# One branch, joined act-table loads and a shorter clear in a convolution, attention and recurrence kernel

## The chip, the cores and the metric

The kernel runs on one core of a Trainium2 chip. The core has five engines with a queue of instructions each: TensorE (PE, matrix products; PEld is its weight load), VectorE (DVE), ScalarE (ACT), GpSimd (POOL) and SyncE (SP, which here issues most DMA transfers). The metric is the device time of one execution in microseconds (us), lower is better. Times of before and after are medians over timed runs; profiles are of one execution each.

## The reference

Input x has 32 images of 128 channels and 64 by 64 positions. Two layers follow each other.

```
# layer 0
x = x + conv3x3(groupnorm(x), kernel mixed per image from 4 kernels)
# layer 1, t = tokens of x, 4096 per image, 128 features
t = t + attn(ln(t))          # 128 -> 16 features, windows of 144 with stride 72, 4 heads,
                             # back to 128, gated, then a layer norm
t = t + ffn(ln(t))

def ffn(x):                  # batch norm over all images, then a recurrence over the tokens
    Wx = x @ W.T
    Wx = (Wx - mean(Wx)) * rsqrt(var(Wx) + 1e-5) * gamma + beta
    y_t = sigmoid(Wx_t + y_(t-1) @ V.T)
```

The mean and variance of the batch norm run over all 32 images, so the recurrence can start only when the last image's `Wx` has its statistics.

## The kernel before

**Start.** Constants are built, image 0 is loaded, and bounds on the inputs are checked on the chip: `okf` says that the attention scores are small enough for an exponential without a maximum, `vm` that the matrix V is contracting enough for the recurrence to be cut into independent runs. Both become integers (`oki` at line 389, `okv` at line 398) and are loaded into registers (lines 426 and 429). The four convolution kernels are loaded into the tiles `k0` by SP at line 318, ahead of the branch; `k0` lives in a pool `first` of its own.

**First branch (line 1984).** If the scores are small, `images` runs, otherwise `images_by_shift`, a slower path that these inputs don't take. `images` works through the 32 images with jobs per image: load (statistics, the mixed kernel `h`), waves (nine buffers `u` of row differences for a fast convolution, on POOL and DVE), taps (transformed kernels `w`), conv (PE products of `w` and `u`), drain, project, feed, values, attend (scores `sc`, exponentials `ex`, weighted values `av`), divide, tail (layer norm and the first result) and last (second layer norm, product with `fWc`, statistics `bnmv`, and the store of the result to `z_d`). Each job is a generator that yields the engine and the tiles that its next step needs. A planner in the kernel keeps a clock of its own (class `Clock`) for each engine; it takes the step that can begin first, and among equals the one with the earliest due time, which the table `DUE` gives per job as (start, length, number of steps) in units of an image. Where the planner expects PE to wait for long, it puts in filler products of `fWc` with itself. So the order of the instructions on all engines follows from the planner's clock and `DUE`. All of these instructions are recorded at line 243.

The tiles `place` (five of 4.6 KB per partition, four of them `k0`) receive kernels, broadcast rows of statistics and squares in turn. In the last image's `last` job the variances are turned into reciprocal deviations on ACT (Ln, Exp), eight products with `fWc` are copied out by ACT (`zt<-nm`), and then PE broadcasts the deviations (`sc<-place,once`) for DVE, which scales and takes the statistics.

**Join, scale, second branch.** Behind the join the batch norm's scale `scl` and shift `shf` are worked out in small steps (lines 1999 to 2011): DVE gathers means and variances, ACT takes the square root, DVE finishes. A second branch (line 2214) takes `by_runs` if V is contracting, otherwise `by_steps`.

**`by_runs`.** Each image's 4096 steps are cut into 128 runs of 32 steps, each warmed up over 16 steps of the run before. Two images form a group, four groups are under way at a time as streams. SP loads the groups' `zr` tiles from `z_d` (line 2033; group 0 lies in `frames` already), DVE builds `dg`, the diagonal of `scl` (line 2041), and clears the state tiles `yw`, two per stream (line 2060). Then each step is a product with V (line 2102), an addition of the input by PE (line 2090) or DVE (line 2108), and a sigmoid (line 2113; the first step of a stream is line 2115). In the warm-up steps only columns 1 to 127 of `yw` are written and read, column 0 stays as cleared. POOL puts the states into `zr`, which is added to the output by DMA.

Of the kernel before, what the change touches and what calls it, by code (L numbers as in the profile page):

```python
# [8 lines left out]
F32 = mybir.dt.float32  # L9
AF = mybir.ActivationFunctionType  # L10
ALU = mybir.AluOpType
AX = mybir.AxisListType

P = 128
# [5 lines left out]
NK = 4  # L20
# [6 lines left out]
GT = NWG * WIN  # L27
# [9 lines left out]
NI = 2  # L37
# [2 lines left out]

SPARE = 0.3, 0.6, 0.6
DUE = {
    "setup": (0.32, 0.08, 8),
    "load": (-0.91, 0.63, 29),
    "taps": (0.02, 0.22, 6),
    "waves": (-0.25, 0.4, 26),
    "conv": (-0.45, 1.09, 36),
    "drain": (-9.0, 0.0, 14),
    "project": (0.75, 0.37, 33),
    "feed": (1.72, 0.61, 27),  # L50
    "values": (1.43, 1.03, 28),
    "attend": (1.15, 1.27, 71),
    "divide0": (1.92, 0.02, 15),
    "divide1": (2.34, 0.02, 11),
# [204 lines left out]
def hybrid_kernel(  # L259
# [24 lines left out]
    nc = tc.nc  # L284
# [17 lines left out]
        return t  # L302


    early = ExitStack()
    first = early.enter_context(tc.tile_pool(name="first", bufs=1))
    inorder = ExitStack()
    inorder.enter_context(tc.manual_schedule())
    tmp = inorder.enter_context(tc.tile_pool(name="tmp", bufs=1))
# [1 line left out]
    frames = const.tile([P, NI, (H + 2) * (W + 2)], F32, name="frames")  # L311
    framed = frames[:, :, 0:T]
    x0 = frames[:, 0].rearrange("p (h w) -> p h w", w=W + 2)[:, 1 : H + 1, 1 : W + 1]
    k0 = [first.tile([P, 9 * P], F32, name=f"place{k}") for k in range(NK)]
    for i in range(2):
        nc.sync.dma_start(x0[:, 32 * i : 32 * i + 32], x[0, :, 32 * i : 32 * i + 32, :])
    for k in range(NK):
        nc.sync.dma_start(k0[k], conv_k[:, k].rearrange("m i j l -> m (i j l)"))

    bdr = tmp.tile([P, DK], F32, name="bdr")  # L320
    ipr = tmp.tile([P, 3 * DK], F32, name="ipr")
# [24 lines left out]

    okf = const.tile([P, 1], F32, name="okf")
    oki = const.tile([P, 1], mybir.dt.int32, name="oki")
    okv = const.tile([P, 1], mybir.dt.int32, name="okv")
    st0 = tmp.tile([P, NBLK, 6], F32, name="st0")  # L350
    mv0 = first.tile([P, 2], F32, name="mv0")
    ps1 = inorder.enter_context(tc.tile_pool(name="ps1", bufs=1, space=bass.MemoryType.PSUM))

    def stats0(i0, i1):
# [31 lines left out]
    smx = tmp.tile([P, 1], F32, name="smx")  # L386
    nc.vector.tensor_reduce(smx, sm, axis=AX.X, op=ALU.max)
    nc.vector.tensor_scalar(okf, smx, 60.0 / HD**-0.5, None, ALU.is_le)
    nc.vector.tensor_copy(oki, okf)
    vr = tmp.tile([P, 1], F32, name="vr")  # L390
    nc.vector.tensor_reduce(vr, va_, axis=AX.X, op=ALU.add)
    vt_ = ps1.tile([P, P], F32, name="vt_")
# [2 lines left out]
    vm = tmp.tile([P, 1], F32, name="vm")  # L395
    nc.vector.tensor_reduce(vm, vt_, axis=AX.X, op=ALU.max)
    nc.vector.tensor_scalar(vm, vm, 1.02, None, ALU.is_le)
    nc.vector.tensor_copy(okv, vm)
    stats0(4, NBLK)
    nc.vector.bn_aggr(mv0, st0.rearrange("p i s -> p (i s)"))  # L400

# [21 lines left out]
    ghalf = const.tile([P, 1], F32, name="ghalf")  # L423
    nc.vector.tensor_scalar_mul(ghalf, gsig, 0.5)
    inorder.close()
    contr = nc.values_load(okv[0:1, 0:1], min_val=0, max_val=1)

    bnmv = const.tile([P, NB, 2], F32, name="bnmv")
    small = nc.values_load(oki[0:1, 0:1], min_val=0, max_val=1)


    QT, NPL, NF, NZ, NU = T // 4, 5, 2, 3, 9
# [1 line left out]
    def images(nc):  # L434
# [6 lines left out]
        with ExitStack() as pa:  # L441
# [26 lines left out]
            def kept(shape, name, fill=None):  # L468
                t = keep.tile(shape, F32, name=name)
                if fill is not None:  # L470
                    nc.gpsimd.memset(t, fill)
                return t
# [18 lines left out]
                nc.vector.tensor_mul(dst, dst, l)  # L491


            places = k0 + [kept([P, 9 * P], f"place{i}") for i in range(NK, NPL)]
            spare = list(places)

            def spread(jobs):
# [139 lines left out]
            def load(b):  # L637
# [11 lines left out]
                taps = []  # L649

                def kernel():
                    if b == 0:
                        taps.append(spare.pop(0))
                        return
                    w = yield from place("SP", ())
                    nc.sync.dma_start(w, conv_k[:, len(taps)].rearrange("m i j l -> m (i j l)"))
                    taps.append(w)
# [679 lines left out]
            def last(b):  # L1337

                while ("x2", b, 0) not in done or (b and ("tail", b - 1) not in done):
                    yield  # L1340
                zt = done["proj", b]

                def product(h):

                    for i in range(4 * h, 4 * h + 4):
                        s = slice(i * BLK, (i + 1) * BLK)
                        yield "PE", nms, (zt[:, s],), (zw[:, s],)
                        ps = clock.take("PE", nms)
                        nc.tensor.matmul(ps, fWc, zt[:, s], start=True, stop=True)
                        yield "ACT", None, (ps,), (zw[:, s],), True  # L1350
                        nc.scalar.copy(zw[:, s], ps)
                        nms.append(ps)

                def third(i):
                    z = zt[:, quarter(i)]

                    def use(w):
                        nc.vector.tensor_mul(z, z, w[:, 0:QT])
                        for j in range(2):
                            nc.vector.bn_stats(st[:, 2 * i + j, :], z[:, BLK * j : BLK * (j + 1)])  # L1360

                    return r_d[b, 2, 1, quarter(i)].partition_broadcast(P), (z,), use

                def straight(i, w):
                    z = zw[:, quarter(i)]
                    zu = z.rearrange("p (g r t) -> p r g t", r=4, t=32)
                    nc.vector.tensor_mul(zu, zu, w)
                    for j in range(2):
                        nc.vector.bn_stats(st[:, 2 * i + j, :], z[:, BLK * j : BLK * (j + 1)])

                got = yield from deviations(zt[:, 0:T], b, 2, True, lambda c: ("x2", b, c))
                st = sml.tile([P, NBLK, 6], F32, name="st3")
                zw = zt
                if b == NB - 1:
                    zw = big.tile([P, T + 8], F32, name="zt")
                    for h in range(2):
                        yield from product(h)
                    yield from beam(got, straight)
                for h in range(2):
                    if b < NB - 1:  # L1380
                        yield from product(h)
                        yield from spread(third(i) for i in (2 * h, 2 * h + 1))
                    yield "SP", None, (zw[:, part(h)],)
                    nc.sync.dma_start(z_d[b, :, part(h)], zw[:, part(h)])
                nc.vector.bn_aggr(bnmv[:, b, :], st.rearrange("p i s -> p (i s)"))
                done["tail", b] = True
# [171 lines left out]
    def images_by_shift():  # L1558

        with ExitStack() as pa:  # L1560
# [126 lines left out]
            def front(b):  # L1687
# [43 lines left out]
                nc.vector.tensor_reduce(cs, co, axis=AX.X, op=ALU.add)  # L1731
                nc.vector.reciprocal(cs, cs)
                nc.vector.tensor_scalar_mul(co, co, cs)
                wb = k0[0].rearrange("p (k m) -> p k m", k=9)
                nc.vector.tensor_scalar_mul(wb, kT[:, 0], co[:, 0:1])
                for k in range(1, NK):
                    nc.vector.scalar_tensor_tensor(
# [28 lines left out]
            def attention(zt):  # L1766
# [25 lines left out]
                for g in range(8):  # L1792
# [77 lines left out]
                        s = slice(GH * i, GH * i + n)  # L1870
                        nc.vector.tensor_add(qs[:, s], qs[:, s], ps[:, i, 0:n])

                    av = k0[2 + q % 2][:, 0:GT]
                    for m0 in range(0, nw, 3):
                        ms = range(m0, min(m0 + 3, nw))
                        ap = av_tile()
# [46 lines left out]
                    for i in range(8):  # L1923
# [2 lines left out]
                            on[:n, i].rearrange("p h f -> p (h f)"),  # L1926
                            ident[:n, :n],
                        )
                    oc = k0[1][:NG5, 0:GT]
                    nc.scalar.copy(  # L1930
                        oc[:, 0:nt].rearrange("p (a b) -> p a b", a=2), ps[:NG5, :, 0 : 4 * n]
                    )
# [48 lines left out]
                tail(b, *cur)  # L1981
                cur = nxt

    with tc.If(small > 0) as arm:
        images(nc)
    with arm.Else():
        images_by_shift()
        for i in range(NI):
            nc.sync.dma_start(framed[:, i], z_d[i])
    early.close()  # L1990


    scl = const.tile([P, 1], F32, name="scl")
    shf = const.tile([P, 1], F32, name="shf")
    bmv = const.tile([P, 2], F32, name="bmv")

    bms = const.tile([P, 6], F32, name="bms")
    bma = const.tile([P, NB], F32, name="bma")
    nc.vector.tensor_copy(bma, bnmv[:, :, 0])
    nc.vector.bn_stats(bms, bma)  # L2000
    nc.vector.bn_aggr(bmv, bms)
    bva = const.tile([P, 1], F32, name="bva")
    nc.vector.tensor_reduce(bva, bnmv[:, :, 1], axis=AX.X, op=ALU.add)
    nc.vector.scalar_tensor_tensor(
        bmv[:, 1:2], bva, 1.0 / NB, bmv[:, 1:2], ALU.mult, ALU.add
    )
    nc.scalar.activation(scl, bmv[:, 1:2], AF.Sqrt, bias=eps)
    nc.vector.reciprocal(scl, scl)
    nc.vector.tensor_mul(scl, scl, fg)
    nc.vector.tensor_mul(shf, bmv[:, 0:1], scl)  # L2010
    nc.vector.tensor_sub(shf, fb, shf)

    def by_runs():

# [2 lines left out]
        with ExitStack() as pb:  # L2017
            zp = pb.enter_context(tc.tile_pool(name="zp", bufs=NSTR + 1))
            hp = pb.enter_context(tc.tile_pool(name="hp", bufs=1))
            p_v = pb.enter_context(tc.tile_pool(name="p_v", bufs=2, space=bass.MemoryType.PSUM))  # L2020
            pb.enter_context(tc.manual_schedule())

            NG = NB // NI
            zs = {}
# [25 lines left out]
            class Stream:  # L2050

                def __init__(self, j):
                    self.j, self.g, self.k, self.phase = j, j, 0, "ACT"
                    self.at = 10.0 * j
                    self.ahead = self.ps = None
                    self.read, self.kept = [-9.0, -9.0], [-9.0, -9.0]
                    self.yw = []
                    for i in range(2):
                        self.yw.append(hp.tile([P, NI, NRUN], F32, name=f"yw{j}_{i}"))
                        nc.vector.memset(self.yw[i], 0.0)  # L2060

                def step(self, k):
                    warm = k < WARM
# [98 lines left out]
    def by_steps():  # L2162

        with ExitStack() as pb:
            fix = pb.enter_context(tc.tile_pool(name="fix", bufs=1))
            io = pb.enter_context(tc.tile_pool(name="io", bufs=2))
            p_s = pb.enter_context(tc.tile_pool(name="p_s", bufs=3, space=bass.MemoryType.PSUM))
            dg = fix.tile([P, P], F32, name="dg")
            nc.vector.tensor_scalar_mul(dg, ident, scl)
            y0 = fix.tile([P, NB], F32, name="y0")  # L2170
# [40 lines left out]
                nc.vector.tensor_add(xk, xk, yk.rearrange("p t b -> p b t"))  # L2211
                nc.sync.dma_start(of[:, :, k * CH : (k + 1) * CH], xk)

    with tc.If(contr > 0) as arm:
        by_runs()
    with arm.Else():
        by_steps()


# [52 lines left out]
```

## Time and profile before

| what | us |
|---|---|
| timed runs | 4437.79, 4440.0, 4445.95 (median 4440.0) |
| the profiled execution | 4430.95 |
| its span, first to last instruction | 4429.2 |
| PE's first convolution product | starts at 36.51 |
| the last image's statistics done | 3877.58 |
| the recurrence's first sigmoid | 3887.83 |
| last copy of POOL before the final DMA | 4399.9 |

A line of the timeline gives the start, the length, the engine, the line, the operation with its output and inputs, and in square brackets how long the engine stood idle before it and what ended that. PE's mean granted clock in this execution is 0.982 of full speed.

### The profile page before, as it was taken

The numbers are of one execution on the slowest core, as the hardware profiler recorded it, in microseconds if no ns is written. First come the engines' busy times: TensorE is split into PE (matmuls) and PEld (weight loads), VectorE is DVE, ScalarE is ACT, GpSimd is POOL, SyncE is SP. The second block draws the span as 40 slices with busy tenths as digits, with TensorE's granted clock in tenths as the row PEclk, the third lists the DMA queues.
The fourth block names the chain that finished last, engine by engine and source line by source line (L and its number), as shares of the span: only waits on it lengthen the run. The fifth ranks groups of instructions, "written<-read, shape, count | busy, mean of one in ns | idle before, by whom it ended". The sixth has DMA issues, their size and how long they took to land.

```text
span 4429.2 us, 103395 instructions
## 1 busy us (share of the span) xinstructions
PE 4151.1 (94%) x42569; PEld 2150.3 (49%) x42569; DVE 3558.9 (80%) x5378; ACT 2423.2 (55%) x3500; POOL 1675.1 (38%) x1654
## 2 busy tenths in 40 slices
PE   6999999999999999999999999999999999889986
PEld 3554544445444544444544545444444445555443
DVE  8788888888888887887887878888888866759884
ACT  1455555555555555555554555555555456467774
POOL 3343333333333333333333333333333422037665
PEclk9999999999999999999999999999999999999998
DMA  3435555545554655555554555555555534459998
GB/s 107 141 116 170 174 177 184 187 166 173 185 168 151 194 174 168 172 180 180 169 179 133 185 171 179 168 168 173 185 185 182 174 119 163 173 204 262 287 264 171
DMA packets 455885, 782.10 MB, mean 177 GB/s; under 512 B 327436, under 2 KB 337380, under 8 KB 422756
## 3 DMA queue, kind: packets, MB, share of 16 engines
q1 hardware_dynamic: 444788, 708.03, 49.0%
q0 software_dynamic: 8704, 67.11, 7.4%
q8 instruction: 339, 5.55, 0.5%
q14 instruction: 150, 1.23, 0.1%
q10 hardware_dynamic: 1904, 0.18, 0.0%
HBM read 494.22 MB, written 274.43 MB: 174 GB/s over the span
## 4 chain that ended last, share of the span: by engine, by line
PE 55%; DVE 21%; DMA 12%; issue 4%; ACT 3%; POOL 2%; SPq 2%; DVEq 0%; ACTq 0%; POOLq 0%
PE nm L243 31%; PE sc L243 12%; PE av L243 9%; DVE zt L243 6%; DVE v L2108 3%; PE v L2102 3%; DVE frames L243 2%; DMA place<-x_d 2%; ACT ex L243 2%; DMA out_dram<-zr 2%; DMA zr<-z_d 2%; DVE u L243 2%; SPq L243 2%; DMA place<-r_d 2%; DVE h L243 2%
## 5 line engine op out<-in xcount | busy, mean ns | idle before, releaser
L243 ACT ACTIVATE ex<-sc 128x1728 f32<-128x1728 f32 x672 | 1081.9, 1610 | 718.9 <-PE sc L243 712.5
L243 POOL TENSOR_TENSOR qe<-qs,mqk 128x576 f32<-128x576 f32 x448 | 615.3, 1376 | 931.4 <-PE sc L243 930.6
L243 PE MATMUL nm<-u,w 128*128 128x512 f32 x1536 | 786.0, 628 | 21.2 <-POOL w L243 18.7
L243 PE MATMUL sc<-qe,ks 32*128 32x432 f32 (+1 forms) x7168 | 667.9, 442 | 33.6 <-ACT ex L243 17.8
L243 PE MATMUL av<-ex,VE 128*32 128x144 f32 x14336 | 620.5, 291 | 21.9 <-DVE avs L243 21.4
L243 PEld LDWEIGHTS av<-ex,VE 128*32 128x32 f32 x14336 | 390.4, 109 | 332.5 <-issue 242.5
L243 PEld LDWEIGHTS sc<-qe,ks 32*128 32x128 f32 x7168 | 285.5, 184 | 414.9 <-issue 185.7
L2102 PE MATMUL v<-yw,fVT 128*128 128x254 f32 (+1 forms) x1504 | 436.3, 429 | 35.5 <-ACT yw L2115 26.1
L243 POOL TENSOR_TENSOR u<-frames 128x528 f32<-128x528 f32 x256 | 383.1, 1505 | 101.5 <-PE nm L243 98.9
L2113 ACT ACTIVATE yw<-v,shf 128x254 f32<-128x254 f32 (+1 forms) x752 | 354.0, 473 | 121.3 <-DVE v L2108 49.4
L2108 DVE SCALAR_TENSOR_TENSOR v<-zr,scl,v 128x256 f32<-128x256 f32 (+1 forms) x585 | 346.2, 659 | 91.7 <-PE v L2102 91.3
L243 PEld LDWEIGHTS nm<-u,w 128*128 128x128 f32 x1536 | 265.4, 192 | 313.5 <-issue 278.3
L243 PE MATMUL nm<-u,h 128*128 128x512 f32 x768 | 399.6, 627 | 0.8 <-DVE frames L243 0.8
L2102 PEld LDWEIGHTS v<-yw,fVT 128*128 128x128 f32 x1504 | 242.0, 194 | 243.5 <-ACT yw L2113 192.1
L243 ACT ACTIVATE place<-zt 128x1024 f32<-128x1024 f32 x256 | 266.5, 1054 | 151.6 <-DVE zt L243 136.1
L243 DVE SCALAR_TENSOR_TENSOR u<-u,u 128x528 f32<-128x528 f32 x256 | 247.9, 982 | 51.9 <-POOL u L243 50.2
L2119 POOL COPY zr<-yw 128x256 f32<-128x256 f32 x416 | 256.2, 728 | 86.8 <-ACT yw L2113 86.2
L243 PE MATMUL nm<-zt,fWc 128*128 128x512 f32 x512 | 273.7, 630 | 3.4 <-ACT zt L243 2.0
L243 PE MATMUL nm<-place,avg 128*32 128x256 f32 x3072 | 237.2, 383 | 12.9 <-ACT place L243 12.6
L243 POOL TENSOR_TENSOR kt<-ks,mqk 128x384 f32<-128x384 f32 (+1 forms) x96 | 88.0, 917 | 389.8 <-ACT ks L243 325.7
L243 ACT COPY zt<-nm 128x512 f32<-128x512 f32 x256 | 149.0, 584 | 152.5 <-PE nm L243 150.6
L243 DVE COPY avs<-av 128x288 f32<-128x288 f32 x224 | 100.8, 450 | 156.5 <-PE av L243 155.6
(226 smaller groups left out, 6417.5 us busy)
## 6 DMA issues: line engine op xcount, KB each, us to landing
place<-r_d SPq DMA_DIRECT2D x380, 512.0 KB
place<-in_conv_k_dram SPq DMA_DIRECT2D x128, 576.0 KB
out_dram<-zt SPq DMA_DIRECT2D x64, 1024.0 KB
z_d<-zt SPq DMA_DIRECT2D x64, 1024.0 KB
x_d<-frames SPq DMA_DIRECT2D x31, 2112.0 KB
place<-x_d SPq DMA_DIRECT2D x124, 528.0 KB
frames<-in_x_dram SPq DMA_DIRECT2D x124, 512.0 KB
zr<-z_d SPq DMA_DIRECT2D x26, 2048.0 KB
```

Of the source, the lines that this page charges most:

```text
L243: got = f(*args, **kw)
L2102: nc.tensor.matmul(self.ps[:, :, c], fVT, self.yw[1 - r % 2][:, :, c], start=not whole, stop=True)
L2108: nc.vector.scalar_tensor_tensor(v, z, scl, v, ALU.mult, ALU.add)
L2113: nc.scalar.activation(y[:, :, c], self.ps[:, :, c], AF.Sigmoid, bias=shf)
L2119: nc.gpsimd.tensor_copy(z, y)
```

## The change

The two flags become one: `vm` is multiplied by `okf` and only the product is turned into an integer. One branch is left, at the end. Its first arm is `images` followed by `by_runs`, its second `images_by_shift` followed by `by_steps`; the scale is worked out at the head of each recurrence in a function `scale`. The pool `first` goes: all five `place` tiles are now the images' own, so image 0's kernels are loaded inside the branch, by the `load` job. ACT's table for the square root is loaded in the last image's `last` job, behind the deviations, and the sigmoid's right behind the square root. Of each `yw` tile only column 0 is cleared. Four rows of `DUE` have other values. (The paths that these inputs don't take get tiles of their own instead of `k0`.)

```diff
 DUE = {
-    "setup": (0.32, 0.08, 8),
+    "setup": (-0.12, 0.02, 8),
-    "waves": (-0.25, 0.4, 26),
-    "conv": (-0.45, 1.09, 36),
+    "waves": (0.02, 0.09, 26),
+    "conv": (-0.35, 1.1, 36),
-    "values": (1.43, 1.03, 28),
+    "values": (1.41, 1.09, 28),
...
-    early = ExitStack()
-    first = early.enter_context(tc.tile_pool(name="first", bufs=1))
...
-    k0 = [first.tile([P, 9 * P], F32, name=f"place{k}") for k in range(NK)]
     for i in range(2):
         nc.sync.dma_start(x0[:, 32 * i : 32 * i + 32], x[0, :, 32 * i : 32 * i + 32, :])
-    for k in range(NK):
-        nc.sync.dma_start(k0[k], conv_k[:, k].rearrange("m i j l -> m (i j l)"))
...
-    mv0 = first.tile([P, 2], F32, name="mv0")
+    mv0 = const.tile([P, 2], F32, name="mv0")
...
-    nc.vector.tensor_copy(oki, okf)
...
-    nc.vector.tensor_copy(okv, vm)
+    nc.vector.tensor_mul(vm, vm, okf)
+    nc.vector.tensor_copy(oki, vm)
...
-    contr = nc.values_load(okv[0:1, 0:1], min_val=0, max_val=1)
-
     bnmv = const.tile([P, NB, 2], F32, name="bnmv")
-    small = nc.values_load(oki[0:1, 0:1], min_val=0, max_val=1)
+    plain = nc.values_load(oki[0:1, 0:1], min_val=0, max_val=1)
...
-            places = k0 + [kept([P, 9 * P], f"place{i}") for i in range(NK, NPL)]
+            places = [kept([P, 9 * P], f"place{i}") for i in range(NPL)]
...
                 def kernel():
-                    if b == 0:
-                        taps.append(spare.pop(0))
-                        return
                     w = yield from place("SP", ())
                     nc.sync.dma_start(w, conv_k[:, len(taps)].rearrange("m i j l -> m (i j l)"))
                     taps.append(w)
...
                 if b == NB - 1:
+                    nc.scalar.preload_act_table_set("sqrt_and_others")
                     zw = big.tile([P, T + 8], F32, name="zt")
...
-    with tc.If(small > 0) as arm:
-        images(nc)
-    with arm.Else():
-        images_by_shift()
-        for i in range(NI):
-            nc.sync.dma_start(framed[:, i], z_d[i])
-    early.close()
...
-    nc.vector.tensor_copy(bma, bnmv[:, :, 0])
...
+    def scale():
+
+        nc.vector.tensor_copy(bma, bnmv[:, :, 0])
+        nc.vector.bn_stats(bms, bma)
+        nc.vector.bn_aggr(bmv, bms)
+        nc.vector.tensor_reduce(bva, bnmv[:, :, 1], axis=AX.X, op=ALU.add)
+        nc.vector.scalar_tensor_tensor(
+            bmv[:, 1:2], bva, 1.0 / NB, bmv[:, 1:2], ALU.mult, ALU.add
+        )
+        nc.scalar.activation(scl, bmv[:, 1:2], AF.Sqrt, bias=eps)
+        nc.scalar.preload_act_table_set("sigmoid_and_others")
+        nc.vector.reciprocal(scl, scl)
+        nc.vector.tensor_mul(scl, scl, fg)
+        nc.vector.tensor_mul(shf, bmv[:, 0:1], scl)
+        nc.vector.tensor_sub(shf, fb, shf)
...
             pb.enter_context(tc.manual_schedule())
+            scale()
...
-                        nc.vector.memset(self.yw[i], 0.0)
+                        nc.vector.memset(self.yw[i][:, :, 0:1], 0.0)
...
-    with tc.If(contr > 0) as arm:
+    with tc.If(plain > 0) as arm:
+        images(nc)
         by_runs()
     with arm.Else():
+        images_by_shift()
         by_steps()
```

More of the change, by code (lines that the diff above doesn't have):

```diff
@@ L348, in hybrid_kernel @@
     oki = const.tile([P, 1], mybir.dt.int32, name="oki")
-    okv = const.tile([P, 1], mybir.dt.int32, name="okv")
     st0 = tmp.tile([P, NBLK, 6], F32, name="st0")
-    mv0 = first.tile([P, 2], F32, name="mv0")
+    mv0 = const.tile([P, 2], F32, name="mv0")
     ps1 = inorder.enter_context(tc.tile_pool(name="ps1", bufs=1, space=bass.MemoryType.PSUM))
@@ L1733, in front @@
                 nc.vector.tensor_scalar_mul(co, co, cs)
-                wb = k0[0].rearrange("p (k m) -> p k m", k=9)
+                wb = one.tile([P, 9, P], F32, name="wb")
                 nc.vector.tensor_scalar_mul(wb, kT[:, 0], co[:, 0:1])
@@ L1871, in attention @@
                         nc.vector.tensor_add(qs[:, s], qs[:, s], ps[:, i, 0:n])
-                    av = k0[2 + q % 2][:, 0:GT]
+                    av = wrk.tile([P, GT], F32, name="avs")
                     for m0 in range(0, nw, 3):
@@ L1928, in attention @@
                         )
-                    oc = k0[1][:NG5, 0:GT]
+                    oc = one.tile([NG5, GT], F32, name="oc")
                     nc.scalar.copy(
@@ L1998, in hybrid_kernel @@
     bma = const.tile([P, NB], F32, name="bma")
-    nc.vector.tensor_copy(bma, bnmv[:, :, 0])
-    nc.vector.bn_stats(bms, bma)
-    nc.vector.bn_aggr(bmv, bms)
     bva = const.tile([P, 1], F32, name="bva")
[L2003 to L2011, printed above, removed]
+    def scale():
[12 more added lines that the diff above has]
+        nc.vector.tensor_sub(shf, fb, shf)
     def by_runs():
@@ L2167, in by_steps @@
             p_s = pb.enter_context(tc.tile_pool(name="p_s", bufs=3, space=bass.MemoryType.PSUM))
+            scale()
             dg = fix.tile([P, P], F32, name="dg")
```

## The prediction

> **What bounds the kernel now.** I read the page's busy shares and its chain first.
>
> ```profile
> PE 4151.1 (94%) x42569; PEld 2150.3 (49%) x42569; DVE 3558.9 (80%) x5378; ACT 2423.2 (55%) x3500; POOL 1675.1 (38%) x1654
> ...
> PE 55%; DVE 21%; DMA 12%; issue 4%; ACT 3%; POOL 2%; SPq 2%; DVEq 0%; ACTq 0%; POOLq 0%
> ```
>
> PE sets the pace for 32 images and then for the recurrence. A change to the seam between these two can only be worth what the seam itself lasts, so I read the timeline there (start, length, engine, line, work, idle time before it and who ended it).
>
> ```profile
> 3871.00 5.20 SPq L243 DMA_DIRECT2D z_d<-zt  x2
> ...
> 3877.21 0.37 DVE L243 BATCH_NORM_AGGREGATE bnmv<-st 128x2 f32<-128x48 f32 x1
> 3881.34 0.18 DVE L1999 COPY bma<-bnmv 128x32 f32<-128x32 f32 x1 [3.76 <-issue]
> 3881.70 13.96 SPq L2033 DMA_DIRECT2D zr<-z_d  x10
> 3883.73 0.19 DVE L2003 TENSOR_REDUCE bva<-bnmv 128x1 f32<-128x32 f32 x1 [2.21 <-issue]
> ...
> 3884.46 0.29 ACT L2007 ACTIVATE scl<-bmv,eps 128x1 f32<-128x1 f32 x1 [14.20 <-DVE bmv L2004]
> ...
> 3885.37 0.16 DVE L2011 TENSOR_TENSOR shf<-fb,shf 128x1 f32<-128x1 f32 x1
> ...
> 3886.20 2.19 DVE L2060 MEMSET yw<- 128x256 f32 x8
> 3886.53 1.28 ACT L2115 ACT_TABLE_LOAD   x1 [1.78 <-DVE yw L2060]
> ...
> 3887.83 0.82 ACT L2115 ACTIVATE yw<-frames,shf,scl 128x254 f32<-128x254 f32 x1
> ```
>
> From the last image's statistics (done at 3877.58) to the first sigmoid (3887.83) pass 10.25 us, in which PE has next to nothing to do. DVE stands for 3.76 and 2.21 us with no wait that the profile shows ("issue"), just behind the end of the first branch. ACT's table load for the sigmoid lies on the path too. Next the stretch before the seam, where one edit puts something new on ACT:
>
> ```profile
> 3858.73 0.42 ACT L243 ACTIVATE place<-place 128x256 f32<-128x256 f32 x1
> 3859.05 1.54 ACT L243 COPY zt<-nm 128x512 f32<-128x512 f32 x3
> ...
> 3859.67 6.25 PE L243 MATMUL nm<-zt,fWc 128*128 128x512 f32 x10 [0.86 <-ACT zt L243]
> ...
> 3865.86 1.15 PE L243 MATMUL sc<-place,once 32*128 32x256 f32 x16
> ...
> 3868.97 1.28 ACT L2007 ACT_TABLE_LOAD   x1 [2.42 <-issue]
> ```
>
> PE waits there for ACT's copies, and the 32x256 products that DVE waits for stand behind PE's. The table load for the square root ran at 3868.97, with ACT idle: it costs nothing now. Last, the start:
>
> ```profile
> 8.82 7.95 SPq L318 DMA_DIRECT2D place<-in_conv_k_dram  x4
> ...
> 16.04 1.28 ACT L421 ACT_TABLE_LOAD   x1 [5.22 <-DMA fWT<-in_ffn_WT_dram]
> ...
> 17.57 0.16 DVE L422 TENSOR_TENSOR gb<-gb,gsig 128x1 f32<-128x1 f32 x1 [0.80 <-ACT gsig L421]
> ...
> 18.46 0.23 DVE L243 TENSOR_SCALAR cp<-ident 128x128 f32<-128x128 f32 x1 [0.67 <-DVE ghalf L424]
> ...
> 18.80 0.15 DVE L243 COPY gm<-nm 128x1 f32<-128x1 f32 x1
> ...
> 26.80 1.75 DVE L243 TENSOR_SCALAR h<-place,co 128x1152 f32<-128x1152 f32 x1
> ```
>
> The four kernel loads are issued long before their first use at 26.80; the path to the first convolution (36.51) runs over DVE's small steps.
>
> **The seam.** Without a join and a second branch, DVE's chain runs on. From the rows of before: bma 0.18 and its gap 0.04, then L2003 to the Sqrt 0.73, Sqrt to the end of shf 1.07: 2.02 us after bnmv. dg (0.29) and one first-column clear (0.06, as the 128x1 memset at the start) bring it to 2.45. On ACT the Sqrt ends at 0.95 + 0.29 = 1.24 and the sigmoid's table load, now right behind it, takes 1.28: 2.52. The first sigmoid starts about 2.55 after bnmv instead of 10.25: **-7.7**. In parts: 5.9 of DVE's idle, 0.3 of the flag's load and branch, 0.2 of clearing (the other seven clears, 1.9 us, already lay beside the table load and ACT's first step, and DVE then idles 14.6 us), 1.3 of table load. The recurrence's own order is the same on PE, POOL and SP, row for row, and on DVE and ACT but for those items; so the 541 us from the first sigmoid to the end move as a block, if its data come along. They do, narrowly: the first zr load, queued on SP behind the z_d stores, can go at 3876.2 (3871.00 + 5.20) instead of 3881.70, 5.5 us earlier, against about 6.7 for the sigmoids. At the 9.8 us that 4.2 MB take at the 430 GB/s moved after 3888, and some 1.5 us from issue to the first bytes, groups 1 to 3 land 4.7, 3.8 and 3.1 us ahead of their first sigmoids (3897.72, 3906.58, 3915.72) now; after the change each margin is 1.2 us smaller, and the last store's 1 MB runs beside the first loads. I take 0, with +1 as the other end.
>
> **The preloads.** The sigmoid's is counted. The square root's moves from idle time to between the Exp (3858.73) and the eight copies, in front of PE's products: all of its 1.28 us can come through, as PE already waits 0.86 for the first copy. PE then runs at a granted clock of 0.50 until about 3863.4, and a later start leaves fewer products in that stretch. Ends 0 and +1.3; I take **+1.0**, nearer the row. The Trainium skill (ScalarE: Activation LUTs, What ACT_TABLE_LOAD costs) gives some 2.7 us with the drain for such a load; by that figure this term would be +2.7, but both loads here show 1.28.
>
> A shorter gap could also spare PE the slow start: the granted clock is 0.50 from 3878 to 3888 and 0.62 to 3896, and the first recurrence steps come every 1.78 us instead of 1.29: four steps, 2.0 us. I take 0 and keep -2.0 as an end: PE still idles about 7.5 us, and at 3857 to 3860 two gaps of 0.81 and 0.86 us were enough for 0.50 behind them. The Trainium skill (TensorE: Matmul & The Clock Gate, Part 1: The HAM clock gate) states that an idle window of about 3.4 us already halves the clock; by that rule 7.5 us of idling keeps the slow start and nothing is gained, while a full clock would make the sum 2.0 lower.
>
> **The start.** The four kernel loads (576 KB each) go behind the branch on SP, ahead of setup's four small loads and of image 1's four. Their room is now tmp's old room: the first waits for the aggregation that ends at 16.61, say 16.8. Issued every 0.43 us they are out at 18.5, when SP reached setup's loads before (18.54), so nothing behind them is issued later. 2.4 MB at the 220 to 430 GB/s seen around there land between 24 and 29; the four uses stand at 26.8, 28.6, about 30.5 and 32.4. The cover is thus a few us; without it DVE stalls up to 2.4, and the taps and PE's first products with it. For this, ACT's small loads no longer queue among the kernel loads: DVE's 0.80 wait for gsig can go, and cp and the reduction beside it now stand behind gm (18.80 to 18.46, 0.34). The flags change by one multiply for one cast (0.0). I take **-1.0**; ends -1.2 and +2.4.
>
> **The order of the images.** New due times reorder all of the 3840 us; no row shows that order, so I count. PE's switches between full, 32-row and 32-column products go from 2737 to 2720: five fewer column to full, seven fewer rows to full, seven more rows to column, twelve fewer full to column. PE's gap at a switch:
>
> ```profile
> 3734.00 0.74 PEld L243 LDWEIGHTS nm<-fWc 128*128 128x128 f32 x6 [0.62 <-issue]
> ...
> 3735.87 0.74 PEld L243 LDWEIGHTS nm<-fWc 128*128 128x128 f32 x6 [0.41 <-issue]
> ```
>
> The first follows score products, the second column products; rows to columns show 0.62 too, full to column at most 0.2, say 0.1. So -5 x 0.41 - 7 x 0.62 + 7 x 0.62 - 12 x 0.1 = -3.3. Behind the last convolution, where fillers stand in for waits, 161 become 151, 0.25 each: -2.5. Together **-5.8**. Waits that a count doesn't show bound it: the stage 2316 to 2435 had 108.7 us of PE work, where 115 is common, at clock 0.94: 6.4 + 7.1 = 13 us lost. One such stage more or less: -19 to +7.
>
> **Sum.** -7.7 + 1.0 - 1.0 - 5.8 = -13.5. The profiled execution took 4430.95 (span 4429.2), 9 below the median 4440.0 of the three timed runs (4437.79 to 4445.95). It becomes 4417.5, and the median **4426.5**. 0.2%, about what a measurement here can tell from no change, is 8.9 us.
>
> **Rivals.**
> (1) Only the seam counts: images and start even, the preload in full: -7.7 + 1.3 = -6.4, 4433.6, inside 0.2%. For it: every term in the images is counted, not seen. Against: both counts fall.
> (2) It doesn't do what it says: DVE's idle is the fetching of new code and stays. The sum loses 5.9: 4432.4, also inside. Against: behind bnmv the code now follows in line, and DVE has no jump there.
> (3) Slower: the waves' due times are squeezed from 0.40 of an image (about 48 us) to 0.09 (11 us), so convolution products wait on PE for a late wave. POOL's differences last 1.5 us each; one late in every second image is 24 us: 4440 - 7.7 + 24 = 4456. It decides from 0.24 us per image (7.7 / 32). Against: measured in attention's steps, convolution starts 0.26 of an image behind POOL's first wave before, 0.25 after, and its end lies 0.33 and 0.34 behind POOL's last.
> (4) The order takes a stage like the one at 2316 away: 13 more, 4413.5.
>
> **Chances.** Forecast 0.45, (4) 0.15, (1) 0.20, (2) 0.06, (3) 0.14. Faster by over 0.2%: 0.60; within: 0.26; slower: 0.14. The range reaches from 4408, a little below (4), to 4447, half of (3); the forecast's own is 4414 to 4436.
>
> **What would show it.** DVE from bnmv to bma without an idle; first sigmoid 2.5 us behind bnmv, and no table load before it; zr loads directly behind the z_d stores; the Sqrt table load ahead of the copies, with PE's wait there near 2 us; first convolution about 35.5; images ending some 6 us sooner against the first convolution. I am wrong if PE's waits for waves grow, or if a gap of several us stays at the seam.

## The result, and the profile after

The changed kernel takes 4409.2 us (median of 4400.2 to 4413.2), the kernel before 4440.4 in the same comparison: ratio 0.9925, 95% interval 0.9906 to 0.9944. That is faster, by about 31 us, where 13.5 were forecast: the time lies inside the stated range (4408 to 4447), the gain is 2.3 times the forecast. The profiled execution took 4413.15 (span 4411.4), 17.8 less than the profiled one of before. Page of the changed kernel, busy shares and chain:

```profile
PE 4148.0 (94%) x42555; PEld 2153.7 (49%) x42555; DVE 3534.8 (80%) x5378; ACT 2428.8 (55%) x3500; POOL 1671.0 (38%) x1654
...
PE 59%; DVE 19%; DMA 11%; ACT 4%; issue 3%; SPq 2%; POOL 1%; DVEq 0%; ACTq 0%; POOLq 0%
```

PE still sets the pace, with nearly the same busy time (4151.1 before); fourteen fewer matmul records are seven fillers of two records each. Timeline of the changed kernel at the start, before the seam and at the seam (start, length, engine, line, work, idle time before it and who ended that):

```profile
16.64 1.83 SPq L243 DMA_DIRECT2D place<-in_conv_k_dram  x4
25.87 1.75 DVE L243 TENSOR_SCALAR h<-place,co 128x1152 f32<-128x1152 f32 x1
...
3842.73 1.28 ACT L243 ACT_TABLE_LOAD   x1
3844.66 6.24 PE L243 MATMUL nm<-zt,fWc 128*128 128x512 f32 x10 [2.28 <-ACT zt L243]
...
3855.89 5.20 SPq L243 DMA_DIRECT2D z_d<-zt  x2
3862.09 0.37 DVE L243 BATCH_NORM_AGGREGATE bnmv<-st 128x2 f32<-128x48 f32 x1
3862.50 0.18 DVE L1983 COPY bma<-bnmv 128x32 f32<-128x32 f32 x1
3863.43 0.30 ACT L1990 ACTIVATE scl<-bmv,eps 128x1 f32<-128x1 f32 x1 [11.90 <-DVE bmv L1987]
3863.74 1.28 ACT L1991 ACT_TABLE_LOAD   x1
3864.93 13.19 SPq L2018 DMA_DIRECT2D zr<-z_d  x10
3865.03 0.82 ACT L2100 ACTIVATE yw<-frames,shf,scl 128x254 f32<-128x254 f32 x1
...
3877.96 0.81 ACT L2100 ACTIVATE yw<-zr,shf,scl 128x254 f32<-128x254 f32 x1 [3.50 <-DMA zr<-z_d]
3879.18 1.22 PE L2087 MATMUL v<-yw,fVT 128*128 128x254 f32 x2 [3.10 <-ACT yw L2098]
```

The seam is as predicted: DVE runs from `bnmv` (ends 3862.46) into `bma` without an idle, and the first sigmoid starts 2.57 us behind `bnmv` instead of 10.25. On both sides of it stands a new loss. PE waits 2.28 us behind the square root's early table load (0.86 before), and the `zr` loads start at 3864.93, behind `bnmv`, though the last `z_d` stores were issued by 3861.09; so ACT waits 3.50 us for group 1 and PE 3.10. What SP waited for ahead of these loads (us in total, times, longest):

```profile
SPq L2018 <- DMA z_d<-zt: 3.5, 1, 3.5
```

By the trace it was the landing of a `z_d` store.

I cut both executions at four marks: PE's first convolution product, the end of the last image's Exp, the end of the last `bnmv`, the first sigmoid.

| stretch, us | before | after | difference | predicted |
|---|---|---|---|---|
| start to first convolution | 36.51 | 35.55 | -1.0 | -1.0 |
| to the last Exp | 3822.6 | 3807.2 | -15.5 | -5.8 |
| to the last `bnmv` | 18.4 | 19.8 | +1.3 | +1.0 |
| to the first sigmoid | 10.25 | 2.57 | -7.7 | -7.7 |
| to the end | 541.4 | 546.4 | +5.0 | 0 |

The long stretch gained most. Engines' busy time over exactly that stretch (window; length; then PE, PEld, DVE, ACT, POOL; last PE's granted clock as a share of full speed, the DMA engines' busy share and GB/s), before and after:

```profile
36.51:3859.15 3822.64, 3659.20 (x40876) 1876.27 (x40876) 3118.82 (x4566) 2044.38 (x2709) 1326.64 (x1095) 0.99 0.52 167
```

```profile
35.55:3842.72 3807.17, 3655.99 (x40862) 1879.55 (x40862) 3096.68 (x4566) 2049.50 (x2708) 1321.99 (x1095) 0.99 0.52 168
```

PE's busy time falls by 3.2, its idle time by 12.3 (163.4 to 151.2). Which waits went, PE's waits between 40 and 3800 us by who ended them (total us, times, longest), before and after:

```profile
PE av L243 <- DVE avs L243: 21.4, 13, 3.9
PE sc L243 <- ACT ex L243: 21.1, 58, 2.2
...
PE sc L243 <- POOL qe L243: 7.2, 5, 2.1
```

```profile
PE sc L243 <- ACT ex L243: 26.2, 60, 1.7
...
PE av L243 <- DVE avs L243: 7.3, 9, 2.1
```

The weighted values' wait for DVE's copies of the last ones falls by 14.1, that for POOL's `qe` by 4.5 (to 2.7); the wait for exponentials grows by 5.1. PE's instructions are the same but for the fillers, so this is a matter of their order. In the six other profiles of the changed order, taken below, the first of these waits stands at 3.5 to 6.7 us.

### The profile page after: what moved, and what is told of

Read it like the earlier page. It is cut to its first block, busy times and chain, and to the rows that moved or that the text cites. A ratio compares the mean times of both kernels' runs of the same rounds, so it can differ in the third digit from the quotient of the medians.

```text
span 4411.4 us, 103365 instructions
## 1 busy us (share of the span) xinstructions
PE 4148.0 (94%) x42555; PEld 2153.7 (49%) x42555; DVE 3534.8 (80%) x5378; ACT 2428.8 (55%) x3500; POOL 1671.0 (38%) x1654
## 4 chain that ended last, share of the span: by engine, by line
PE 59%; DVE 19%; DMA 11%; ACT 4%; issue 3%; SPq 2%; POOL 1%; DVEq 0%; ACTq 0%; POOLq 0%
PE nm L243 33%; PE sc L243 13%; PE av L243 10%; DVE zt L243 5%; DVE v L2093 3%; DMA zr<-z_d 3%; ACT ex L243 2%; DVE frames L243 2%; PE v L2087 2%; SPq L243 2%; DMA out_dram<-zr 2%; DVE u L243 1%; DMA place<-r_d 1%; DVE h L243 1%; DVE cp L243 1%
## 5 line engine op out<-in xcount | busy, mean ns | idle before, releaser
L243 PE MATMUL nm<-u,w 128*128 128x512 f32 x1536 | 776.1, 624 | 22.1 <-POOL w L243 18.3
L243 PE MATMUL nm<-u,h 128*128 128x512 f32 x768 | 388.2, 619 | 0.8 <-DVE frames L243 0.8
L243 DVE SCALAR_TENSOR_TENSOR zt<-sc,gbk,zt 128x576 f32<-128x576 f32 (+1 forms) x192 | 174.5, 909 | 44.1 <-PE sc L243 43.6
L243 PEld LDWEIGHTS nm<-u,h 128*128 128x128 f32 x768 | 129.2, 188 | 143.1 <-issue 136.6
```

Source lines behind the costliest of these rows:

```text
L243: got = f(*args, **kw)
```

## The experiments

Times are compared with runs of the kernel before on the same chip; its median lay at 4436.1 beside the first four runs (the changed kernel again, the two halves, both late edits), 4439.4 beside the next four and 4428.7 beside the last four. The planner's order is fixed when the kernel is built, so switches (of PE between full, 32-row and 32-column products) and fillers are counted there. "The planner's own clock" is the value that the kernel's class `Clock` holds for DVE when the last image has been placed.

### Where the gain is: due times, the kernels' place, the one branch

**The changed kernel again.**

> The changed kernel once more, as the measure for the others of this group. If the time is a property of the program, it comes out 25 to 35 us under the kernel before (0.9922 to 0.9944), the stretch from the first convolution to the end of the last image's Exp again about 3807 us. If the first comparison was a lucky chip, the gap falls to the 18 us that the two profiled executions showed, or to the 13.5 of the prediction.

4409.7 against 4436.1, ratio 0.9940 (0.9926 to 0.9954): 26 us. Its stretch to the last Exp is 3804.7. The gap is a property of the program.

**Only the due times, on the kernel before** (the four rows of the change, nothing else).

> The kernel before with nothing but the four new rows of due times. Theory A (the order of the images carries what the prediction missed): 15 to 28 us under the kernel before; first convolution to end of the last Exp near 3807 us, the seam still 10.25 us from bnmv to the first sigmoid. Rival B (the counts of switches and fillers were right, the missing part comes from the structure: the one branch, the kernels' places): about 6 us under the kernel before. Rival C (squeezed waves cost, hidden by the rest): slower than before.

**Only the structure: the changed kernel with the old due times.**

> The changed kernel with the old due times: the structure alone. Theory A: seam -7.7, start -1.0, Sqrt load +1.4, late zr load +5.0, together 2 us under the kernel before, which this measurement can't tell from no change. Rival B: 20 us or more under the kernel before, images near 3810 us in spite of the old order. The recurrence (first sigmoid to end) should be about 546 us, as in the changed kernel, under both.

Theory A and rival B fell. The first run took 4497.2 (1.0150, 1.0129 to 1.0171), the second 4501.8 (1.0149, 1.0131 to 1.0167): each half of the change alone costs 60 us or more, and together they win 26 to 31. The loss lies in the images: 3891.9 and 3893.0 to the last Exp (3822.6 before). Rival C had forecast a slower first run; it is slower, but not for the reason given: the list of PE's waits names no wave `u` in its profile, as in none of the others. The structure must change the order itself. Comparing the builds shows how: in the changed kernel image 0's four kernel loads are steps of a job, which the planner times, and from the first steps on it takes other choices. So the next run takes this one part of the structure and the due times together.

```diff
-    k0 = [first.tile([P, 9 * P], F32, name=f"place{k}") for k in range(NK)]
...
-    for k in range(NK):
-        nc.sync.dma_start(k0[k], conv_k[:, k].rearrange("m i j l -> m (i j l)"))
...
-            places = k0 + [kept([P, 9 * P], f"place{i}") for i in range(NK, NPL)]
+            places = [kept([P, 9 * P], f"place{i}") for i in range(NPL)]
...
-                    if b == 0:
-                        taps.append(spare.pop(0))
-                        return
```

(and the four new rows of due times; the pool `first` goes too)

> The kernel before, with two of the change's edits together: image 0's four kernel loads go into the branch, and the four rows of due times are the new ones. Two branches, the join and the whole clears stay. Built, its order of the images is that of the changed kernel, instruction for instruction on PE, DVE, POOL and SP (ACT: without the square root's early load). Theory A (the gain is this order, and the one branch is worth little net): 20 to 26 us under the kernel before, 4410 to 4416; first convolution to the last Exp near 3807 us, Exp to statistics about 17 us, seam 10.25, first sigmoid to end 541; the changed kernel then is only about 0 to 4 us better. Rival B (the one branch itself makes the images faster): images back near 3822 us, about 4435.

4405.8 against 4439.4, ratio 0.9932 (0.9912 to 0.9951): 34 us, the whole gain, with two branches, the join and the whole clears still there. PE's products of the images stand in the same order in both traces. To the last Exp it takes 3798.5, with PE idle for 143.6 us of it:

```profile
35.93:3834.48 3798.55, 3654.91 (x40862) 1878.53 (x40862) 3094.50 (x4566) 2049.14 (x2709) 1317.19 (x1095) 0.99 0.53 168
```

Its seam, in the timeline:

```profile
3850.73 0.37 DVE L243 BATCH_NORM_AGGREGATE bnmv<-st 128x2 f32<-128x48 f32 x1
3854.84 0.18 DVE L1990 COPY bma<-bnmv 128x32 f32<-128x32 f32 x1 [3.74 <-issue]
3854.93 0.18 DVE L1994 TENSOR_REDUCE bva<-bnmv 128x1 f32<-128x32 f32 x1
...
3859.08 0.82 ACT L2106 ACTIVATE yw<-frames,shf,scl 128x254 f32<-128x254 f32 x1
```

The first idle of DVE is there as before, the second (2.1 to 2.2 in three other profiles with a join) is missing: 7.98 from `bnmv` to the sigmoid. Theory A is right: due times and kernel loads belong together and carry the gain; the one branch, net, is worth nothing that this measurement shows. The stretches say the same: from the last Exp to the end this run takes 568.0 us, the changed kernel 568.7 and 570.4 in its two profiles.

### What an order is worth

Is the new order a better one by its design, or one pick out of many? Three runs move one row of the changed kernel, one a row of the kernel before.

```diff
-    "attend": (1.15, 1.27, 71),
+    "attend": (1.16, 1.27, 71),
```

> The changed kernel, with one due time that the change didn't touch moved by 0.01 of an image (attend 1.15 to 1.16, 1.2 us). The order differs from PE's row 152 of the images on; fillers 534 instead of 481, switches 2723 instead of 2720. Theory F (a filler is 0.25 us of PE and stands for a wait that is 0.6 filled, so 0.42 us each): 22 us slower than the changed kernel. Theory P (the planner's own clock at the images' end, 3747.9 against 3735.1 us, tells): 13 us slower. Rival (such a small shift does nothing, and only the change's rows matter): within 4 us of the changed kernel.

The next two put back one row of the change each:

```diff
-    "waves": (0.02, 0.09, 26),
+    "waves": (-0.25, 0.4, 26),
```

> The changed kernel with the old row for waves alone. Fillers 522, switches 2689, the planner's own clock at the images' end 3787.7 against 3735.1. Theory F: 17 us slower than the changed kernel. Theory P: 53 us slower. By switches alone (31 fewer) it would be some 10 us faster.

```diff
-    "setup": (-0.12, 0.02, 8),
+    "setup": (0.32, 0.08, 8),
```

> The changed kernel with the old row for setup alone, a job that ends before image 2. Fillers 677, switches 2722, the planner's own clock 3800.3 against 3735.1. Theory F: 82 us slower than the changed kernel. Theory P: 65 us slower. Rival (setup's row only matters at the start): 0 to 3 us.

And the shift of attend by 0.01, on the kernel before:

> The kernel before, with attend's due time moved by 0.01 of an image (1.15 to 1.16) and nothing else. Fillers 627 instead of 488, the planner's own clock 3798.5 against 3707.8. Theory (both kernels' rows are a fitted pick out of a scatter of orders, and any step off it falls back into the scatter): 20 to 85 us slower than the kernel before. Rival (the kernel before has an ordinary order, and the change found a better one): as likely faster as slower, within 20 us.

Against the kernel before they took 1.0052 (1.0035 to 1.0069), 1.0093 (1.0068 to 1.0117), 1.0121 (1.0095 to 1.0146) and 1.0146 (1.0128 to 1.0164): by the ratios (0.9940 for the changed kernel) the first three are 50, 68 and 80 us slower than it, the last is 65 slower than the kernel before (60 by the medians). Of the change's other two rows, values does nothing: built with its old value, the planner makes the same order. The row conv was not run alone. All orders that ran, over the stretch to the last Exp:

| order | fillers | switches | planner's clock | stretch | PE busy | PE idle |
|---|---|---|---|---|---|---|
| changed kernel | 481 | 2720 | 3735.1 | 3807.2 | 3656.0 | 151.2 |
| before | 488 | 2737 | 3707.8 | 3822.6 | 3659.2 | 163.4 |
| changed, attend +0.01 | 534 | 2723 | 3747.9 | 3850.2 | 3676.1 | 174.1 |
| changed, old waves | 522 | 2689 | 3787.7 | 3868.5 | 3680.3 | 188.1 |
| before, attend +0.01 | 627 | 2762 | 3798.5 | 3879.9 | 3700.6 | 179.2 |
| before, new due times | 587 | 2693 | 3791.9 | 3891.9 | 3701.6 | 190.3 |
| changed, old due times | 713 | 2708 | 3820.3 | 3893.0 | 3717.8 | 175.2 |
| changed, old setup | 677 | 2722 | 3800.3 | 3894.4 | 3715.7 | 178.7 |

A shift of 1.2 us in one due time costs 43 us in the changed kernel's images and 57 in those of before. Each of the six steps off these two orders that ran, the kernels' move included, loses 43 to 87 us: both kernels sit at a favourable point of a scatter some 90 us wide, as far as six steps can show it. Switches don't tell: the fewest (2689) stand in a slow order. Fillers tell part, through PE's busy time: for the changed kernel with old due times the group of fillers is

```profile
L243 PE MATMUL nm<-fWc 128*128 128x128 f32 x1408 | 205.2, 289 | 0.1
```

against

```profile
L243 PE MATMUL nm<-fWc 128*128 128x128 f32 x944 | 141.4, 293 | 0.3 <-DVE VT L243 0.3
```

in the changed kernel, both over the stretch: 63.8 us, as much as the 61.8 by which PE is busier (a filler is two records, so 141.4 us over 472 fillers is 0.30 each; nine more stand behind the last Exp). The idle time beside them, 12 to 39 us, isn't in any count. The theory on fillers gave 22, 17 and 82 us for the first three runs, that on the planner's clock 13, 53 and 65, where 50, 68 and 80 were measured: one hits the last, the other comes near the second, and both give less than half of the small shift. The planner's clock separates good from bad, but puts before 27 us ahead of after, the wrong way round. What makes an order good stays open beyond this: the fast ones have less idle time on PE, which can be read behind a run and not ahead of it.

### What the seam gives back

Two edits of the changed kernel, together and each alone. The first zr tile gets a pool of its own, opened first:

```diff
+            z1 = pb.enter_context(tc.tile_pool(name="z1", bufs=1))
-            zp = pb.enter_context(tc.tile_pool(name="zp", bufs=NSTR + 1))
+            zp = pb.enter_context(tc.tile_pool(name="zp", bufs=NSTR))
...
-                        zs[g] = zp.tile([P, NI, NRUN, RUN], F32, name="zr")
+                        zs[g] = (z1 if g % (NSTR + 2) == 1 else zp).tile([P, NI, NRUN, RUN], F32, name="zr")
```

and the square root's early load goes:

```diff
-                    nc.scalar.preload_act_table_set("sqrt_and_others")
```

Both:

> The changed kernel without the early table load for the square root, and with the first zr tile in a pool of its own, in room that the images' big tiles never used. Theory (the first zr load waits for that room's last readers, not for its data): it is issued right behind the z_d stores, about 3.8 us earlier against bnmv, PE's second wait at the recurrence's start (3.10 us) goes, first sigmoid to end 546.4 to about 541.5; PE's wait behind the Exp 2.28 to 0.9; but the square root's table load goes to the seam, where ACT idles (0 us), or onto the path (+1.3). Together 5 to 6.4 us under the changed kernel. Rival (the load is late because of the stores' landing or SP itself): issue stays 2.5 us behind bnmv and only 1.4 us are won.

4398.9 (4393.9 to 4412.3) beside the changed kernel's 4409.7 on the same chip; against before 0.9919 (0.9903 to 0.9936). Its median lies below those of both kernels, though one of its six executions is as slow as the changed kernel. Exp to `bnmv` 16.7 instead of 19.6, first sigmoid to end 542.7 instead of 548.3: in these two stretches 8.5 us, more than the 5 to 6.4 expected, as the early load proved dearer than its 1.4 us of waiting.

The pool alone:

> The changed kernel with the first zr tile in a pool of its own, the square root's early load kept. Theory (the late zr load costs the recurrence 5 us by itself): zr loads begin behind the z_d stores instead of 2.5 us behind bnmv, first sigmoid to end 541 to 543 instead of 546 to 548, 4 to 6 us under the changed kernel's 4409.5, Exp to statistics still 19.6 us. Rival (the two costs are one: the early load's delay of the last stores makes the zr loads late): first sigmoid to end stays at 546.

4399.3, 0.9937 (0.9924 to 0.9950). Its timeline:

```profile
3845.96 0.33 SPq L243 DMA_DIRECT2D z_d<-zt  x1
3846.88 0.32 SPq L2019 DMA_DIRECT2D zr<-z_d  x1
3850.84 0.32 SPq L243 DMA_DIRECT2D z_d<-zt  x1
3851.20 13.74 SPq L2019 DMA_DIRECT2D zr<-z_d  x9
...
3864.71 0.82 ACT L2101 ACTIVATE yw<-zr,shf,scl 128x254 f32<-128x254 f32 x1
```

Group 1's two `zr` loads now go between and right behind the last two `z_d` stores, before `bnmv` (3852.54), and its sigmoid waits for nothing. The other eight, in the shared pool, still wait for a store to land and start at 3860.29, in time for all but waits under 1 us. First sigmoid to end is 542.6, though Exp to `bnmv` stays at 20.9: the two costs are separate. By that stretch the late load cost 3.3 to 5.7 us (546.0 to 548.3 in the four profiles of this order with it, 542.6 and 542.7 in the two without); the medians of this group (4401.5 for the kernel with whole clears below) lie too near each other to show it.

No early load, alone:

> The changed kernel without the early table load for the square root alone. Theory: Exp to statistics 16.7 instead of 19.6 us (PE's second wait and its slow stretch go with the load), the load moves to ACT's idle time before bnmv, the seam stays 2.57, first sigmoid to end stays 546 to 548: 3 us under the changed kernel. By the prediction's +1.0: 1 us. Rival (the load then lies on the path in front of the square root): seam 3.9, nothing won.

4395.1 (4388.9 to 4407.4), 0.9923 (0.9909 to 0.9937); next to that spread the gain is read from the stretches. Exp to `bnmv` 16.65, seam 2.57, first sigmoid to end 547.2: the table load went back to ACT's idle time (3844.90) and the rival is refuted. Its two lines of the timeline, PE's ten products and ACT's load:

```profile
3839.70 4.56 PE L243 MATMUL nm<-zt,fWc 128*128 128x512 f32 x10 [0.85 <-ACT zt L243]
...
3844.90 1.28 ACT L1989 ACT_TABLE_LOAD   x1
```

With the early load the products took 6.24 in the changed kernel and 7.42 in the run with the pool alone. In the changed kernel's windows the granted clock is halved behind the wait:

```profile
3844.72:3846.72 2.00, 2.00 (x3) 0.96 (x4) 0.00 (x0) 0.87 (x2) 0.00 (x0) 0.50 1.03 434
3846.72:3848.72 2.00, 2.00 (x5) 0.79 (x4) 0.00 (x0) 0.94 (x2) 0.00 (x0) 0.66 0.99 418
```

So in this order the early load costs 1.4 us of waiting, and 1.5 to 2.9 more where the clock falls. It doesn't always: in the run with whole clears below PE waited the same 2.28 us and the products took 4.56.

Whole clears again:

```diff
-                        nc.vector.memset(self.yw[i][:, :, 0:1], 0.0)
+                        nc.vector.memset(self.yw[i], 0.0)
```

> The changed kernel with the recurrence's buffers cleared whole again. By the prediction: the first clear is 0.2 us longer on DVE, of which 0.1 reaches the first sigmoid (ACT's table load ends 0.07 us later than DVE's part), the other seven lie beside ACT's and PE's first steps: seam 2.6 to 2.8, time the same as the changed kernel's within 1 us. Rival (the clears hold back the first steps): seam 4.4.

4401.5, 0.9939 (0.9924 to 0.9954), as the changed kernel. The seam, timeline:

```profile
3859.28 2.19 DVE L2045 MEMSET yw<- 128x256 f32 x8
3859.62 0.84 ACT L2100 ACTIVATE yw<-frames,shf,scl 128x254 f32<-128x254 f32 x1
```

Again 2.57 from `bnmv` (3857.05): ACT's table load ends last, and the clears lie beside it. The shorter clear is worth nothing.

## Why the prediction was right in sign and half in size

- **The seam, -7.7: right,** by its chain of small steps to 0.02 us. Of its parts "0.2 of clearing" is 0: with whole clears the sigmoid starts at the same 2.57. Rival (2), that DVE's idle stays, is refuted; what the idle at the join was, no run shows.
- **The start, -1.0: right** (-0.96); the kernels' cover held, first use at 25.87.
- **The zr loads, "I take 0, with +1 as the other end": wrong, +5.0.** The step that failed is "the first zr load, queued on SP behind the z_d stores, can go at 3876.2". The load went 3.84 us after the last store was issued (3861.09 to 3864.93), when a store had landed. I looked at the data and at SP's queue, not at the room: the tile's pool spans memory of the images' tiles. That it is the room and not the stored data is shown by the run with a pool of its own, where group 1's loads didn't wait and the loss was gone.
- **The square root's early load, +1.0 with an end of +1.3: too small.** Between the two profiles it shows +1.3, but the stretch of before held a halved clock too (18.4; 16.6 to 16.7 in the five other profiles without the load). Against those the changed order's profiles with the load stand 1.4 to 4.3 higher, 2.9 on average. The Trainium skill (ScalarE: Activation LUTs, What ACT_TABLE_LOAD costs) adds a drain of 1.38 us to the load's 1.28; here the first copy starts at 3844.02, 0.01 behind the load, so no drain shows. That the total came near the page's 2.7 has another cause, PE's clock.
- **The clock at the recurrence's start, 0: nearly right.** PE idled 8.33 us, and its first products took 1.17 and 1.01 us where 0.61 follow later; two slow steps came instead of three, some 0.6 us less. The reason given, that two short gaps were enough for a clock of 0.50, was weak: of the six profiles with the short wait only that of before shows it. The rule weighed there (the Trainium skill, TensorE: Matmul & The Clock Gate, Part 1: The HAM clock gate) said so too; but at the early load the clock fell behind waits of 0.81 and 2.28 us with 1.12 us of products between them, no one of them as long as its 3.4.
- **The order of the images, -5.8: the mis-sized term.** -15.5 between the two profiles; over the seven profiled executions of this order the stretch lies at 3796.1 to 3807.2, mean 3802.5, so -20 against the one profile of before. The step that failed is taking the counted switches and fillers for the whole term. The waits, which I bounded (-19) instead of costing, gave 12.3 net: 14.1 at one edge, `av` behind `avs`, while others grew. PE's busy time fell by 3.2, near the count, but that is luck: the fillers, priced at -2.5, took 141.7 us before and 141.4 after (ten fewer behind the last convolution, three more ahead of it), while the products of `u` and `w` fell from 786.0 to 776.1 and others rose. What the switches gave no run shows by itself. Rival (4), one slow stage less, is not what happened: of 32 equal parts of the stretch, seven had more than 8 us of PE idle before and six after; the part with the stage at 2316 went from 11.2 to 6.5, but others rose. Rival (3), squeezed waves, lost: no wait of PE for `u` shows in either profile, and the old row put back costs 68 us. Yet the four new rows without the kernels' move were 61 us slower, so the sign hangs on the rows and the structure together.
- **The sum.** In profile terms -13.5 stands against -17.8: -9.7 too little from the order, +5.3 missed at the preload and the zr loads. The other 13 us of the measured 31 come from carrying the sum over to the median: the profiled execution of before was 9.5 below its median, that of after 4 above. Executions of one program differ that much: the four of the changed kernel span 4400.2 to 4413.2. How much of these 13 us belongs to the order, no run splits. Rival (1), "only the seam counts", has it upside down: the seam's 7.7 is given back (2.9 at the early load on average, 5.0 at the zr loads), and the order stands for all that is measured.

## What to carry to other kernels

When an order comes from a greedy planner, its tuning belongs to exactly the program it was made on: moving four loads or one due time by 1 us may cost more than the edit can win, so compare the built orders before crediting an edit, and run a few neighbouring tunings before judging it. Cost a new order by the waits on the bounding engine and not only by its work; where no trace has them, the honest range is the width of the scatter. When a stretch is shortened, ask of each load in it what memory it writes and who read that last, and keep a preload out of any place where the bounding engine already waits.

## What the runs showed of the hardware

- PE's clock behind short waits varied from execution to execution. With the early load PE waited 2.28 us ahead of the ten 128x512 products in seven profiles and 1.73 in one; in six of the eight the granted clock stood at 0.50 there, for 3.41 us in four (3844.67 to 3848.08 in the changed kernel) and 6.83 in two, and the products took 6.04 to 7.42 us against 4.56 at full clock. Of the six profiles with a wait of 0.31 to 0.86 one had the slow clock.
- At the end of a branch DVE stood 3.7 us before its first instruction in all four profiles with a join; a second one of 2.1 to 2.2 us came in three of the four. Without the join both are gone.
- Executions of one program roughly follow the mean granted clock: in the run with both edits 4412.3 at 0.980, 4402.9 at 0.981, 4395.4 to 4400.0 at 0.982, 4393.9 at 0.983. Which of the two sets the other no run shows.
